# Field-pair products: packed W, end-aligned chunks, one transposed x, and 5120 small memsets on GpSimd

## The chip, the cores and the metric

The kernel runs on one core of one Trainium2 chip. The metric is the device time of one execution in microseconds (us). Engines are named as the profile names them: PE is TensorE's matmul side and PEld its weight loads, DVE is VectorE, ACT is ScalarE, POOL is GpSimd, SP is SyncE. A core has 16 DMA engines.

## The reference

For every batch row there are F = 32 fields of D = 64 numbers. For each of the 496 pairs of fields i < j, field i is multiplied by that pair's own 64 x 64 matrix, and the result is multiplied, element by element, with field j.

```python
i_idx, j_idx = np.triu_indices(32, k=1)          # 496 pairs
vi, vj = inputs[:, i_idx, :], inputs[:, j_idx, :]
vdotw = jnp.einsum('bpd,pde->bpe', vi, W)        # W: (496, 64, 64)
y = (vdotw * vj).reshape(4096, 496 * 64)         # all float32
```

The output has 4096 x 31,744 numbers, 520 MB; x is 33.5 MB and W 8.1 MB.

## The kernel before, in words

The batch is cut into 32 tiles of 128 rows, and everything is done tile by tile (loop over `t`). A tile of x is loaded on ACT's DMA queue into one of two buffers (`load_x`, L82), one tile ahead. TensorE transposes it in two halves of eight 128 x 128 blocks (`transpose_x`, L102), and ScalarE copies each half from PSUM into `xT`, of which there are two (L103). The halves of the next tile are transposed at pairs 5 and 6 of the current one (`PREFETCH_AT`), both halves of the first tile before the loop.

The fields are taken in twos. "Pair p" in the code is fields 2p and 2p + 1, held in the upper and lower 64 partitions of one transposed block. For field i all its products with fields j > i are one wide matmul with (31 - i) x 64 columns. W is packed on the host accordingly: two halves of rows, one for even and one for odd fields. It is loaded on SP's queue in 16 loads into 16 buffers, one for each pair (L115).

A pair's columns are cut from the left into chunks of at most 512. Each chunk takes two of the eight PSUM banks (`take_banks(2)`, four chunks are in flight), one bank for each of the two fields; two matmuls fill them (L145). VectorE multiplies them with the matching columns of x and writes into the output ring. Where it can, one instruction handles both fields as two runs of columns (`runs`, L155); near the ends there is one instruction per field (L164). Because x's matching columns differ by 64 between the two fields, the two runs of x start 64 columns apart.

The ring has 28,160 columns of SBUF for 31,744 output columns of a tile. Each tile makes four stores on SP's queue (`STORES`, L170) of 7552, 6528, 7872 and 9792 columns, in this order; a store's place in the ring is free again when it has landed. The instructions stand on each engine in the order in which the loops name them; waits between engines, and of an engine on its own earlier results, are derived from overlaps of what is read and written.

Of the kernel before, what the change touches and what calls it, by code (L numbers as in the profile page):

```python
# [1 line left out]

# [6 lines left out]

F32 = mybir.dt.float32  # L10
ALU = mybir.AluOpType

P = 128
BANK = 512
BANKS = 8
CHUNK = BANK

STORES = [[0, 1], [2, 3], [4, 5, 6], [7, 8, 9, 10, 11, 12, 13, 14, 15]]
PREFETCH_AT = [5, 6]
RING = 28160  # L20


@with_exitstack
def pair_bilinear_kernel(
    ctx: ExitStack,
    tc: tile.TileContext,
    x: bass.AP,
    w: bass.AP,
    out: bass.AP,
    F: int,  # L30
    D: int,
):

    nc = tc.nc
    B = x.shape[0]
    NT = B // P
    NPR = F // 2

    width = [(F - 1 - i) * D for i in range(F)]
    off = [sum(width[:i]) for i in range(F)]
    woff = [sum(width[0 : 2 * p : 2]) for p in range(NPR)]  # L60
    store_w = [sum(width[2 * p] + width[2 * p + 1] for p in g) for g in STORES]

    const = ctx.enter_context(tc.tile_pool(name="const", bufs=1))
    xtpool = ctx.enter_context(tc.tile_pool(name="xT", bufs=2))
    psum = ctx.enter_context(tc.tile_pool(name="ps", bufs=1, space=bass.MemoryType.PSUM))

    ident = const.tile([P, P], F32, tag="ident", name="ident")
    make_identity(nc, ident)

    def runs(tl, a, b, n):  # L70

        ap = tl[:, a : a + n]
        return bass.AP(ap.tensor, ap.offset, [list(ap.ap[0]), [b - a, 2], list(ap.ap[1])])


    xbuf = [const.tile([P, (F + 1) * D], F32, tag=f"x{b}", name=f"x{b}") for b in range(2)]
    for xb in xbuf:
        nc.gpsimd.memset(xb[:, F * D :], 0.0)  # L78

    def load_x(t):  # L80
        xt = xbuf[t % 2]
        nc.scalar.dma_start(out=xt[:, : F * D], in_=x[ts(t, P), :])  # L82
        return xt

    pring = psum.tile([P, BANKS * BANK], F32, tag="pring", name="pring")
    bank = 0

    def take_banks(n):

        nonlocal bank  # L90
        if bank + n > BANKS:
            bank = 0
        got = pring[:, bank * BANK : (bank + n) * BANK]
        bank = (bank + n) % BANKS
        return got

    def transpose_x(xT, t, xt, g):

        n = 2 * BANK // P
        pt = take_banks(2)  # L100
        for c in range(n):
            nc.tensor.transpose(pt[:, ts(c, P)], xt[:, ts(n * g + c, P)], ident)  # L102
        nc.scalar.copy(xT[:, ts(g, 2 * BANK)], pt)  # L103

    def new_xT(t):
        return xtpool.tile([P, NPR * P], F32, tag="xT", name=f"xT_{t}")

    ring = const.tile([P, RING], F32, tag="ring", name="ring")
    at = 0
    xs = {0: load_x(0)}  # L110

    w_sb = []
    for p in range(NPR):
        wp = const.tile([P, width[2 * p]], F32, tag=f"w{p}", name=f"w{p}")
        nc.sync.dma_start(out=wp, in_=w[:, woff[p] : woff[p] + width[2 * p]])  # L115
        w_sb.append(wp)

    xTs = {0: new_xT(0)}
    for g in range(2):
        transpose_x(xTs[0], 0, xs[0], g)  # L120

    for t in range(NT):
        xt, xT = xs.pop(t), xTs.pop(t)
        if t + 1 < NT:
            xs[t + 1] = load_x(t + 1)
        for s, group in enumerate(STORES):
            if at + store_w[s] > RING:
                at = 0
            osb = ring[:, at : at + store_w[s]]
            at += store_w[s]  # L130
            o0 = off[2 * group[0]]
            for p in group:
                if t + 1 < NT and p in PREFETCH_AT:
                    if t + 1 not in xTs:
                        xTs[t + 1] = new_xT(t + 1)
                    transpose_x(xTs[t + 1], t + 1, xs[t + 1], PREFETCH_AT.index(p))
                for c0 in range(0, width[2 * p], CHUNK):
                    n = [max(0, min(CHUNK, width[2 * p + h] - c0)) for h in range(2)]
                    half = -(-n[0] // BANK) * BANK
                    pm = take_banks(2 * half // BANK)  # L140
                    for b0 in range(0, n[0], BANK):
                        b1 = min(b0 + BANK, n[0])
                        for h in range(2):
                            if b0 < n[h]:
                                nc.tensor.matmul(  # L145
                                    pm[:, h * half + b0 : h * half + b1],
                                    xT[h * D : (h + 1) * D, ts(p, P)],
                                    w_sb[p][h * D : (h + 1) * D, c0 + b0 : c0 + b1],
                                    start=True,
                                    stop=True,  # L150
                                )
                    o = [off[2 * p + h] - o0 + c0 for h in range(2)]
                    xj = [(2 * p + h + 1) * D + c0 for h in range(2)]
                    if n[1] > half - BANK and o[1] + n[0] <= store_w[s]:
                        nc.vector.tensor_tensor(  # L155
                            runs(osb, o[0], o[1], n[0]),
                            runs(pm, 0, half, n[0]),
                            runs(xt, xj[0], xj[1], n[0]),
                            ALU.mult,
                        )  # L160
                    else:
                        for h in range(2):
                            if n[h]:
                                nc.vector.tensor_tensor(  # L164
                                    osb[:, o[h] : o[h] + n[h]],
                                    pm[:, h * half : h * half + n[h]],
                                    xt[:, xj[h] : xj[h] + n[h]],
                                    ALU.mult,
                                )
            nc.sync.dma_start(out=out[ts(t, P), o0 : o0 + store_w[s]], in_=osb)  # L170


# [33 lines left out]
```

## Time and profile before

The median of 12 runs is 1337.9 us (1337.49 to 1338.22). The profiled execution took 1338.14 us, of which the profile's span is 1336.3.

| engine | instructions | busy us | share of span |
|---|---|---|---|
| PE (matmul) | 5376 | 1142.5 | 85% |
| PEld (weight load) | 5376 | 490.5 | 37% |
| DVE | 1344 | 1199.1 | 90% |
| ACT | 65 | 66.1 | 5% |
| POOL | 8 | 0.9 | 0% |

| DMA queue | packets | MB |
|---|---|---|
| q1: stores and W, issued by SP | 20,736 | 528.49 |
| q10: x, issued by ACT | 4608 | 33.56 |
| q8 and q14: instructions | 59 | 0.83 |

Busy time is what an engine spends inside instructions; a share below 100% doesn't say whether the rest was waiting for something that matters. The mean rate of all DMA is 421 GB/s over the span. GpSimd does nothing after the first 1.5 us, in which it makes the identity matrix for the transposes and clears 64 spare columns behind each x buffer.

The page counts 13,084 instructions with semaphore and DMA-issuing ones. Beside the page's groups, the trace keeps for every DMA packet its start, its duration, its size and its queue, but not which of the 16 DMA engines carried it. That can be followed, since one engine's packets follow each other within a few ns.

### The profile page before, as it was taken

What the parts mean: (1) busy time and instruction counts of PE and PEld (TensorE: products, weight loads), DVE (VectorE), ACT (ScalarE), POOL (GpSimd) and SP (SyncE); (2) the same over time, 40 slices, a digit from 0 to 9 for tenths busy, and PEclk for the clock granted to TensorE, in tenths of its full rate; (3) what the DMA queues carried; (4) which work ended last, traced back from release to release, by engine and by line L of the source; (5) the groups of instructions that cost most, each with busy time, mean ns of one, the idle gap of its engine ahead of it and who ended that gap; (6) DMA issues with size and microseconds to landing.
All of it is one profiled execution on the core that took longest, in us unless ns stands there. A gap on an engine that the chain in (4) does not pass through costs nothing. (4 is left out here: it accounts for less than half of the span.)

```text
span 1336.3 us, 13084 instructions
## 1 busy us (share of the span) xinstructions
PE 1142.5 (85%) x5376; PEld 490.5 (37%) x5376; DVE 1199.1 (90%) x1344; ACT 66.1 (5%) x65; POOL 0.9 (0%) x8
## 2 busy tenths in 40 slices
PE   7888888888988889888888899888888888888883
PEld 3333333333333333333333343333333333333331
DVE  5999998988999999899999999989988989999994
ACT  1000000000000000000000000000000000000000
POOL 0000000000000000000000000000000000000000
PEclk9999999999999999999999999999999999999997
DMA  9999999999999999999999999999999999999998
GB/s 393 431 428 430 427 425 426 414 427 430 408 426 426 414 432 426 419 421 420 427 434 413 424 404 443 423 426 411 430 429 415 426 421 415 426 426 430 418 421 368
DMA packets 25403, 562.88 MB, mean 421 GB/s; under 512 B 2944, under 2 KB 3328, under 8 KB 4864
## 3 DMA queue, kind: packets, MB, share of 16 engines
q1 hardware_dynamic: 20736, 528.49, 92.6%
q10 hardware_dynamic: 4608, 33.56, 6.0%
q8 instruction: 42, 0.69, 0.2%
q14 instruction: 17, 0.14, 0.0%
HBM read 41.94 MB, written 520.09 MB: 421 GB/s over the span
## 5 line engine op out<-in xcount | busy, mean ns | idle before, releaser
L155 DVE TENSOR_TENSOR ring<-pring,x 128x1024 f32<-128x1024 f32 (+3 forms) x1088 | 1154.4, 1107 | 117.3 <-DMA out_dram<-ring 70.9
L145 PE MATMUL pring<-w,xT 64*128 64x512 f32 (+4 forms) x4864 | 1074.8, 553 | 145.7 <-DVE ring L155 141.3
L145 PEld LDWEIGHTS pring<-w,xT 64*128 64x128 f32 x4864 | 432.2, 185 | 761.8 <-DVE ring L155 668.3
L103 ACT COPY xT<-pring 128x1024 f32<-128x1024 f32 x64 | 64.8, 1012 | 1197.5 <-PE pring L102 1197.5
L102 PE MATMUL pring<-ident,x 128*128 128x128 f32 x512 | 72.7, 288 | 29.3 <-DMA x<-in_x_dram 28.7
L102 PEld LDWEIGHTS pring<-ident,x 128*128 128x128 f32 x512 | 58.3, 147 | 65.1 <-issue 65.1
L164 DVE TENSOR_TENSOR ring<-pring,x 128x64 f32<-128x64 f32 (+4 forms) x256 | 71.1, 299 | 3.3
L103 ACT ACT_TABLE_LOAD x1 | 1.3, 1283 | 1.7 <-PEq L198 1.7
masks.py:199 POOL TENSOR_SCALAR_AFFINE_SELECT ident<-ident 128x128 f32<-128x128 f32 x1 | 0.3, 294 | 0.0
L78 POOL MEMSET x<- 128x64 f32 x2 | 0.2, 152 | 0.0
masks.py:197 POOL MEMSET ident<- 128x128 f32 x1 | 0.2, 205 | 0.3 <-POOLq L198 0.3
L198 POOL MEMSET const-bfloat16-1.0<- 128x1 bf16 x1 | 0.1, 102 | 0.0
L198 POOL MEMSET const-uint8-127<- 128x1 uint8 x1 | 0.1, 102 | 0.0
L198 POOL MEMSET const-float32-0.0<- 128x1 f32 x1 | 0.1, 99 | 0.2 <-issue 0.2
L198 POOL MEMSET const-float32-1.0<- 128x1 f32 x1 | 0.1, 99 | 0.0
## 6 DMA issues: line engine op xcount, KB each, us to landing
out_dram<-ring SPq DMA_DIRECT2D x32, 4896.0 KB, 18.6
out_dram<-ring SPq DMA_DIRECT2D x32, 3936.0 KB, 17.3
out_dram<-ring SPq DMA_DIRECT2D x32, 3776.0 KB, 19.0
out_dram<-ring SPq DMA_DIRECT2D x32, 3264.0 KB, 19.4
x<-in_x_dram ACTq DMA_DIRECT2D x32, 1024.0 KB, 17.6
w<-in_w_dram SPq DMA_DIRECT2D x1, 992.0 KB, 7.7
w<-in_w_dram SPq DMA_DIRECT2D x1, 928.0 KB, 12.0
w<-in_w_dram SPq DMA_DIRECT2D x1, 864.0 KB, 13.7
```

Of the source, the lines that this page charges most:

```text
L78: nc.gpsimd.memset(xb[:, F * D :], 0.0)
L102: nc.tensor.transpose(pt[:, ts(c, P)], xt[:, ts(n * g + c, P)], ident)
L103: nc.scalar.copy(xT[:, ts(g, 2 * BANK)], pt)
L145: nc.tensor.matmul(pm[:, h * half + b0 : h * half + b1], xT[h * D : (h + 1) * D, ts(p, P)], w_sb[p][h * D : (h + 1) * D, c0 + b0 : c0 + b1 ...
L155: nc.vector.tensor_tensor(runs(osb, o[0], o[1], n[0]), runs(pm, 0, half, n[0]), runs(xt, xj[0], xj[1], n[0]), ALU.mult,)
L164: nc.vector.tensor_tensor(osb[:, o[h] : o[h] + n[h]], pm[:, h * half : h * half + n[h]], xt[:, xj[h] : xj[h] + n[h]], ALU.mult,)
L198: nc = bacc.Bacc("TRN2", target_bir_lowering=False, num_devices=1)
```

## The change

- W goes into one buffer, packed so that the odd field's columns are shifted by 64, and is loaded in five loads of all rows (pairs 0; 1; 2 and 3; 4 to 6; 7 to 15).
- The chunks of a pair are aligned at their ends: the short chunk comes first, then chunks of 512. With the shift, both fields' chunk lies over the same columns of x, and the instruction reads x once for both runs (a step of 0 between the runs). The first chunk's 64 extra columns of the odd field land in ring columns that the pair's last chunk overwrites later. The spare columns behind x are gone.
- There is one transposed x. Its second half is made at pair 3 of the same tile, its first half at pair 9 of the tile before.
- GpSimd writes one spare column, 128 x 1 numbers, four times for each chunk: 40 chunks x 32 tiles x 4 = 5120 memsets. Nothing reads the column.

```diff
-PREFETCH_AT = [5, 6]
+LOADS = [[0], [1], [2, 3], [4, 5, 6], [7, 8, 9, 10, 11, 12, 13, 14, 15]]
+FIRST_HALF_AT, SECOND_HALF_AT = 9, 3
...
-    woff = [sum(width[0 : 2 * p : 2]) for p in range(NPR)]
+    woff = [i % 2 * D + sum(width[i % 2 : i : 2]) for i in range(F)]
...
+    xT = const.tile([P, NPR * P], F32, tag="xT", name="xT")
+    spare = const.tile([P, 1], F32, tag="spare", name="spare")
...
-    for p in range(NPR):
-        wp = const.tile([P, width[2 * p]], F32, tag=f"w{p}", name=f"w{p}")
-        nc.sync.dma_start(out=wp, in_=w[:, woff[p] : woff[p] + width[2 * p]])
+    w_sb = const.tile([P, sum(width[0::2])], F32, tag="w", name="w")
+    for g in LOADS:
+        upto = woff[2 * g[-1]] + width[2 * g[-1]]
+        nc.sync.dma_start(out=w_sb[:, done:upto], in_=w[:, done:upto])
+        done = upto
+    transpose_x(xbuf[0], 0)
...
-                if t + 1 < NT and p in PREFETCH_AT:
-                    transpose_x(xTs[t + 1], t + 1, xs[t + 1], PREFETCH_AT.index(p))
-                for c0 in range(0, width[2 * p], CHUNK):
+                if p == SECOND_HALF_AT:
+                    transpose_x(xt, 1)
+                if p == FIRST_HALF_AT and t + 1 < NT:
+                    transpose_x(xbuf[(t + 1) % 2], 0)
+                first = (width[2 * p] - 1) % BANK + 1
+                for c1 in range(first, width[2 * p] + 1, BANK):
+                    n = first if c1 == first else BANK
+                    c0 = c1 - n
+                    odd = width[2 * p + 1] and c1 > D
+                    pm = take_banks(2)
+                    for _ in range(4):
+                        nc.gpsimd.memset(spare, 0.0)
...
-                    if n[1] > half - BANK and o[1] + n[0] <= store_w[s]:
+                    o = [off[2 * p + h] - o0 + c0 - h * D for h in range(2)]
+                    if odd and (c0 or c1 < width[2 * p]):
                         nc.vector.tensor_tensor(
-                            runs(osb, o[0], o[1], n[0]),
-                            runs(pm, 0, half, n[0]),
-                            runs(xt, xj[0], xj[1], n[0]),
+                            runs(osb, o[0], o[1], n),
+                            runs(pm, 0, BANK, n),
+                            bass.AP(xj.tensor, xj.offset, [xj.ap[0], [0, 2], xj.ap[1]]),
                             ALU.mult,
                         )
```

On the engines: POOL gets 5119 memsets in a row after the identity matrix and one before its last step, each waiting for the one before it; no other engine waits for them. SP issues 11 DMAs less. DVE has 43 products per tile instead of 42.

## The prediction

> **What bounds the kernel now.** I began with the page's slices and its table of DMA queues, because they say whether any engine can be the limit at all.
>
> ```profile
> PE 1142.5 (85%) x5376; PEld 490.5 (37%) x5376; DVE 1199.1 (90%) x1344; ACT 66.1 (5%) x65; POOL 0.9 (0%) x8
> DMA  9999999999999999999999999999999999999998
> q1 hardware_dynamic: 20736, 528.49, 92.6%
> q10 hardware_dynamic: 4608, 33.56, 6.0%
> q8 instruction: 42, 0.69, 0.2%
> ```
>
> No compute engine is full; the 16 DMA engines are, from the first slice to the last but one. 528.5 MB (the output, and W once) and 33.6 MB of x are moved at 421 GB/s. The next question is whether VectorE still has a say. Its timeline of one batch tile and the waits answer that:
>
> ```profile
> 230.89 0.21 DVE L164 TENSOR_TENSOR ring<-pring,x 128x64 f32<-128x64 f32 x1
> 233.65 9.00 DVE L155 TENSOR_TENSOR ring<-pring,x 128x1024 f32<-128x1024 f32 x8 [2.55 <-DMA out_dram<-ring]
> 242.57 0.54 DVE L164 TENSOR_TENSOR ring<-pring,x 128x192 f32<-128x192 f32 x2
> ...
> 255.65 0.23 DVE L164 TENSOR_TENSOR ring<-pring,x 128x64 f32<-128x64 f32 x1
> ```
> ```profile
> DVE ring L155 <- DMA out_dram<-ring: 70.9, 35, 3.0
> ```
>
> Once per tile VectorE stops for some 2.5 us, before the third store group, until the previous tile's largest store has landed. Then it needs 22.2 us (233.65 to 255.87) for groups three and four and issues the next largest store. This is a loop: landing, 22.2 us of products, issue, landing 18.6 us later (the page's median for that store is of this size). It turns in 41 us. Is the loop paced by VectorE or by the transfers? The trace's packet records decide. The sum over one DMA engine per tile is eight rows of each store and of x:
>
> ```
> packet bytes  15 DMA engines  the 16th, while compute runs  the 16th after 1322 us
> 26112          968 ns          982 to 1020 ns
> 30208         1119 ns         1133 to 1161 ns
> 31488         1166 ns         1166 to 1218 ns
> 39168         1448 ns         1472 to 1500 ns                1448 ns
>  8192 (x)      309 ns          309 to 326 ns
> ```
>
> Fifteen engines need 8 x (968+1119+1166+1448+309) = 40.1 us per tile (39.95 us with the 3.5 ns by which packets overlap). The sixteenth needs 0.98 us more. Following its packets end to start, it has work at every tile boundary: it finishes about 3 us after the others, which run dry for about 0.8 us just before the largest store is issued. 39.95 + 0.98 = 40.93 us against issues 41.0 us apart. **One stretched DMA engine paces the program**; the others idle, and VectorE waits.
>
> What stretches it? Its excess comes in steps of about 9.4 ns, 31.7 us over the run, or 2.4 ns for each of the page's 13,084 instructions. By phase of the tile it is 1.6 to 1.9% where 7.5 to 9 instructions start per us, and 3.3 to 3.5% where the transposes bring 13 per us; the correlation over 20 phases is 0.75. After 1322 us, with no instruction left, its packets have full speed. [...]
>
> [...] 9.4 ns per step and 2.4 ns per instruction are four instructions to a step. [...] PE's 10,752 instructions make the 42 packets of q8 (16,384 bytes, 0.95 us each); the other engines fetch 8192 bytes, 309 ns. [...] VectorE here reads PSUM and x; no row of before has GpSimd beside it, so the trace can't say. [...] beside x, a 39,168-byte packet takes 1766 ns, 318 more, one x packet.
>
> **The change, part by part.**
>
> *GpSimd's memsets.* 40 chunks x 32 tiles x 4 = 5120. Nobody reads the spare column, so nothing waits for it. But they are 5120 more records: 5120 x 2.4 ns = **12.3 us** on the pacing engine. Bounds: 0 (if only other engines' records count) and 14 us (at 2.73 ns, the dearest tenth of the run). I take 12.3. Each memset waits for the one before. POOL's bare rows take 99 ns; a wait on its own engine's previous instruction costs VectorE 187 ns of start to start (below), so 0.2 us is likely, 1.0 ms in all. Bounds 0.035 us (POOL's rows start that close without waits) and more than 0.261 us, where 5120 of them outlast the 1336 us span and POOL becomes the bound.
>
> *Their fetch.* 5120 x 64 B (PE's 0.69 MB by 10,752) is 40 packets of 8192 bytes at 309 ns, 12.4 us of one engine. If they are on any engine but the sixteenth they fit in its 0.98 us per tile plus what the sixteenth loses too: 0. On the sixteenth: 12.4 more. Spread over all: 0.8. I take 0, the others are in the range. Two fetches 657 us apart (317 and 974 us; by their spacing SP's) lie on the sixteenth, PE's do not, so engines seem to have their own places.
>
> *W in five loads.* Eleven loads fewer, and with them 11 x 8 rows per DMA engine and 11 completion packets of 9 ns. A packet costs 9 ns over its bytes less the 3.5 overlap: 88 x 5.5 + 99 ns = **-0.6 us** on every engine. SP's 11.6 us of waits between W issues go, but the queue never ran dry there (W's packets end at 27.7 us, the first store was issued at 24.9), so that is worth 0. A coarser load makes pair 3 and pairs 5, 6, 8 to 15 wait for their group: by bytes at 430 GB/s the last lands at 27 us, and pair 7 is first multiplied near 40 us. 0.
>
> *One transposed x.* The transposes keep their number (512) and their copies (64, 1012 ns). Eight instead of sixteen come before the first matmul: the first product starts some 0.6 us earlier; the DMA is busy with W then, so 0. The second half is made at pair 3, before VectorE's wait, the first half of the next tile at pair 9, twelve us later than x's landing, so PE's 28.7 us of waits for x shrink. PE is ahead by four buffers and VectorE waited for it only 17.3 us, 13.4 at the start. On ACT's queue the x load stands ahead of the copy of pair 3, as it did before pair 5. 0.
>
> *Chunks aligned at the end.* VectorE gets 43 instead of 42 instructions a tile and 64 columns less. What matters is the wait on itself. The chain of waits shows it:
>
> ```profile
> 1281.30 4.49 DVE ring L155 x4
> 1285.78 0.04 DVEq L155
> 1285.82 0.04 issue
> 1285.86 3.49 DVE ring L155 x3
> ```
>
> After a short two-run chunk the next instruction waits for its end: a start to start of 1185 ns for 896 columns, 252 ns over the columns' 933, where other chunks have 65 over. So 187 ns, ten times a tile. In the new order the short chunk comes first and the waiting one is the pair's last: for pairs 0 to 6 it is two or three places behind, done by then; only pairs 8, 9, 10 wait at once. In groups three and four eight waits become three: 5 x 0.187 = 0.94 us off VectorE's 22.2 us. Two more instructions (65 ns each) and 128 columns less (133 ns) cancel. That would shorten the loop if VectorE paced it. It doesn't: the cover is the sixteenth engine, which has some 2 us of queue when the largest store is issued. Worth 0 here; VectorE's wait grows by 0.94 + 0.4 us a tile instead.
>
> **Sum.** The profiled run took 1338.14 us (span 1336.3 and 1.84 around it): 1338.14 + 12.3 - 0.6 = 1349.8. The median of the runs, 1337.9, lies 0.24 lower: **1349.6 us**.
>
> **Rivals.**
>
> *B, no change:* POOL's records cost the pacing engine nothing, say because the stretching comes from PE's own instructions (its rate correlates at 0.80). For it: PE makes 82% of all instructions, so the trace can hardly part them. Then 1337.9 - 0.6 = 1337.3.
>
> *C, faster:* VectorE's loop is the bound after all and my packet chain is wrong. The idle stretches of the DMA engines at tile ends sum to 15 us (engine-time over 16, start and tail left out). With 0.94 us less per tile, 30 us over 32 tiles, they close: 1338 - 15 = 1323. It decides if the sixteenth engine is idle at all when the largest store is issued. Against it: its 40.93 of 41.0 us. With the memsets' cost on top, some 1323 to 1336.
>
> *D, slower still:* the fetch is on the pacing engine, 1349.6 + 12.4 = 1362; or each memset takes 0.3 us and POOL ends at 1536; or GpSimd holds VectorE up by 99 ns for each of 43 instructions, 4.3 us a tile, more than its 2.5 + 1.3 of slack, 0.5 x 32 = 16 over 1338.
>
> **How the numbers follow.** The forecast 0.72, within 1346 to 1354; B 0.10; C 0.09; D 0.09. About 0.2% (2.7 us) is what a measurement can tell from no change. Slower 0.81, same 0.10, faster 0.09. The range takes in B and D's lower part: 1337 to 1357.
>
> **What would show it.** Right: POOL some 0.5 ms busy over about 1 ms, the instruction queues 40 packets richer, tile issues 41.4 to 41.5 us apart while memsets run and 41.0 after, the sixteenth engine's packets 3.5 to 4% long instead of 2.4, VectorE's wait for stores from 71 to 110 us or more. Wrong: 41.0 us apart throughout with memsets running (B), 40.5 (C), or PE and VectorE waiting for POOL or a second late DMA engine (D).

## The result, and the profile after

The changed kernel takes 1354.21 us (median of 7 runs, 1354.1 to 1354.4), the kernel before 1337.88 (29 runs): a ratio of 1.0122, interval 1.0113 to 1.0132. So the change costs 16.3 us, where 11.7 were forecast. The profiled execution took 1354.32 us, its span is 1352.5.

From the page of the kernel after: counts and busy time of each engine, two rows of slices, the DMA queues.

```profile
PE 1162.8 (86%) x5376; PEld 553.9 (41%) x5376; DVE 1183.2 (87%) x1376; ACT 66.1 (5%) x65; POOL 507.7 (38%) x5126
POOL 6666666666666666666666640000000000000000
DMA  9999999999999999999999999999999999999998
q1 hardware_dynamic: 19152, 528.49, 91.6%
q10 hardware_dynamic: 4608, 33.56, 5.9%
q8 instruction: 42, 0.69, 0.2%
q14 instruction: 58, 0.48, 0.1%
L146 POOL MEMSET spare<- 128x1 f32 x5120 | 507.1, 99 | 295.1
```

POOL is the only row that is new. Its 5120 memsets of 99 ns have 157 ns from start to start, because each waits for the one before it, and end in slice 24, at 803 us. The bytes of the two data queues are the same, in 1584 fewer packets, and the share of the DMA engines' time that they took barely moves. The bound is where it was: DMA at 9 in every slice but the last.

The end of the memsets at 803 us splits the program in two, and two stretches can be compared with the same stretches of before. First the kernel before, then the kernel after (from:to, length, then busy time of PE, PEld, DVE, ACT and POOL, granted TensorE clock, DMA share, GB/s):

```profile
52.00:804.00 752.00, 655.09 (x3080) 279.75 (x3076) 687.96 (x770) 36.44 (x36) 0.00 (x0) 1.00 0.99 423
845.00:1296.00 451.00, 391.93 (x1850) 167.92 (x1848) 411.85 (x462) 22.27 (x22) 0.00 (x0) 1.00 0.99 423
```
```profile
52.00:804.00 752.00, 653.35 (x3028) 312.41 (x3026) 665.92 (x775) 36.45 (x36) 474.96 (x4795) 0.96 0.98 416
845.00:1296.00 451.00, 397.59 (x1848) 189.29 (x1846) 405.73 (x472) 22.27 (x22) 0.00 (x0) 0.96 0.99 422
```

While memsets run, 416 GB/s are moved instead of 423; afterwards 422. The loss is all in the first stretch. The packet records say it in time. Each tile's largest store starts 41.74 us after that of the tile before it over the first 18 tiles, and 40.85 us over the rest; before it was 40.97 and 40.73. The clock is lower after, 0.96 in both stretches, so with memsets and without; the DMA doesn't follow it.

One engine's packets carry the loss. Summed over the run, the packets of the pacing engine are 46.9 us longer than those of the other fifteen, against 31.7 before: 4.3 us for each 100 us while memsets run, 2.3 to 2.4 afterwards, as much as before.

The timeline of VectorE over one tile of the kernel after (start, length, what ran, and in brackets the wait ahead of it), and its waits for stores (total, times, longest):

```profile
229.14 3.49 DVE L159 TENSOR_TENSOR ring<-pring,x 128x1024 f32<-128x1024 f32 x3
237.29 9.07 DVE L159 TENSOR_TENSOR ring<-pring,x 128x896 f32<-128x896 f32 x9 [4.67 <-DMA out_dram<-ring]
...
258.47 2.21 DVE L159 TENSOR_TENSOR ring<-pring,x 128x896 f32<-128x896 f32 x2
```
```profile
DVE ring L159 <- DMA out_dram<-ring: 120.0, 46, 5.0
```

VectorE's wait ahead of group three is 4.67 us instead of 2.55, and 120.0 instead of 70.9 us in all. From the end of the wait to the end of group four, where the largest store is issued, it is about 21.3 us (237.29 to 258.6), where it was 22.2. VectorE became quicker, and waits longer.

### The profile page after: what moved, and what is told of

Read it like the earlier page. It is cut to its first block, busy times and chain, and to the rows that moved or that the text cites. A ratio compares the mean times of both kernels' runs of the same rounds, so it can differ in the third digit from the quotient of the medians.

```text
span 1352.5 us, 18254 instructions
## 1 busy us (share of the span) xinstructions
PE 1162.8 (86%) x5376; PEld 553.9 (41%) x5376; DVE 1183.2 (87%) x1376; ACT 66.1 (5%) x65; POOL 507.7 (38%) x5126
## 4 chain that ended last, share of the span: by engine, by line
DMA 50%; DVE 33%; issue 9%; PE 6%; POOL 0%; DVEq 0%; ACT 0%; POOLq 0%
DMA out_dram<-ring 50%; DVE ring L159 29%; PE pring L149 6%; DVE ring L167 5%; POOL spare L146 0%; PE pring L107 0%; DVEq L159 0%; ACT xT L108 0%; DVEq L198 0%; POOL ident masks.py:199 0%; DVEq L167 0%; POOL ident masks.py:197 0%; POOLq L194 0%
## 5 line engine op out<-in xcount | busy, mean ns | idle before, releaser
L149 PE MATMUL pring<-w,xT 64*128 64x512 f32 (+4 forms) x4864 | 1100.8, 569 | 161.7 <-DVE ring L159 151.1
L159 DVE TENSOR_TENSOR ring<-pring,x 128x1024 f32<-128x1024 f32 (+3 forms) x1056 | 1104.2, 1106 | 150.3 <-DMA out_dram<-ring 120.0
L149 PEld LDWEIGHTS pring<-w,xT 64*128 64x128 f32 x4864 | 498.4, 194 | 721.8 <-DVE ring L159 534.7
L146 POOL MEMSET spare<- 128x1 f32 x5120 | 507.1, 99 | 295.1
L167 DVE TENSOR_TENSOR ring<-pring,x 128x64 f32<-128x64 f32 (+3 forms) x320 | 97.4, 354 | 1.2 <-DMA out_dram<-ring 0.9
L107 PEld LDWEIGHTS pring<-ident,x 128*128 128x128 f32 x512 | 55.5, 142 | 57.1 <-DVE ring L159 48.8
```

The lines of the kernel that those rows point to most:

```text
L146: nc.gpsimd.memset(spare, 0.0)
L149: nc.tensor.matmul(pm[:, h * BANK : h * BANK + n], xT[h * D : (h + 1) * D, ts(p, P)], w_sb[h * D : (h + 1) * D, a : a + n], start=True, st ...
L159: nc.vector.tensor_tensor(runs(osb, o[0], o[1], n), runs(pm, 0, BANK, n), bass.AP(xj.tensor, xj.offset, [xj.ap[0], [0, 2], xj.ap[1]]), ALU ...
L167: nc.vector.tensor_tensor(osb[:, o[h] + h * D : o[h] + n], pm[:, h * (BANK + D) : h * BANK + n], xj[:, h * D :], ALU.mult,)
```

## The experiments

In all of them "+" and "-" are against the kernel named, and the kernel before ran beside each at 1337.5 to 1337.9 us. Two runs part the memsets from the rest of the change. Theory R of the expectations: every instruction on record in the trace makes the packets of one DMA engine, the one that paces the program, longer, by 2.4 ns on average in the kernel before (31.7 us / 13,084).

**1. The change without memsets.**

```diff
-    spare = const.tile([P, 1], F32, tag="spare", name="spare")
...
-                    for _ in range(4):
-                        nc.gpsimd.memset(spare, 0.0)
```

> The changed kernel without its memsets. Theory R [...]: only the eleven saved W loads are left, 1337.3 us, 0.6 below before; that engine's excess is back to about 32 us. Rival L (the rest of the change costs something too, since 16.3 us were measured for 12.3 forecast): 1340 to 1342 us. Rival C (VectorE's loop paced the kernel before): the shorter loop shows now, 1323 to 1330 us.

Measured: 1338.23 us against 1337.65, ratio 1.0004 (0.9996 to 1.0012). Packed W, aligned chunks and the single transposed x are together worth nothing that shows. VectorE's waits and its largest group in this kernel:

```profile
DVE ring L156 <- DMA out_dram<-ring: 105.2, 41, 4.1
L156 DVE TENSOR_TENSOR ring<-pring,x 128x1024 f32<-128x1024 f32 (+3 forms) x1056 | 1104.4, 1111 | 135.2 <-DMA out_dram<-ring 105.2 <-PE pring L146 19.1
```

The wait for stores is 105.2 us with no memset in the program: it took in what VectorE had gained. That ends rival C: a shorter VectorE loop is not a shorter program. The clock was 0.967 here too, so the memsets don't lower it.

**2. The kernel before, plus memsets.** The same two edits, added to the kernel before.

> The kernel before with the 5120 memsets alone, four for each chunk as in the changed kernel. Theory R: 1337.9 + 5120 x 3.0 ns (the stretch of the pacing engine's packets grew from 31.7 to 46.9 us in the changed kernel) = 1353 us. Rival L: 12.3 us from the memsets, 1350. If the records did nothing: 1338.

Measured: 1354.08 us, ratio 1.0123 (1.0109 to 1.0136): +16.4. The pacing engine's packets were 46.7 us long over the others'. The 16.3 us of the change are the memsets' alone, and the layout around them doesn't matter.

**3. Half of them.** `range(4)` becomes `range(2)`: 2560 memsets.

> The changed kernel with two memsets for each chunk, 2560 instead of 5120, each the same. Theory R: the cost is by the number, so half: 1345.5 to 1346 us, and GpSimd is done after 402 us. A rival in which the mere presence of a busy GpSimd costs [...] would keep the cost per us of GpSimd's activity too, so this run tells R only from a fixed cost (1354 us) and from a threshold (1338 us).

Measured: 1345.96 us, ratio 1.0062 (1.0048 to 1.0076), 7.7 us over experiment 1. The group of memsets:

```profile
L146 POOL MEMSET spare<- 128x1 f32 x2560 | 253.5, 99 | 147.5
```

They end at 402 us. The excess of the pacing engine is 4.3 to 4.4 us per 100 us up to there and 2.3 afterwards. The same rate for half as long, so half the cost.

**4. No wait between memsets.** 128 spare columns take turns, so that a memset depends on none of the recent ones.

```diff
+    spare = const.tile([P, 128], F32, tag="spare", name="spare")
...
+                        nc.gpsimd.memset(spare[:, turn : turn + 1], 0.0)
+                        turn = (turn + 1) % 128
```

> The changed kernel with the 5120 memsets going round 128 spare columns, so that none has to wait for the one before. The number of instructions is the same. Theory R with one record for each instruction: the cost is the same, 1353 to 1354 us, though GpSimd is done far sooner (157 ns apart with the wait, perhaps 35 to 100 without). If the wait or its semaphore is what makes a memset dearer (3.0 ns) than the average instruction before (2.4 ns): 1350 us. If cost follows the time in which GpSimd is active: 1342 to 1347 us.

Measured: 1352.74 us, ratio 1.0113 (1.0099 to 1.0126), 14.5 over experiment 1. POOL's slices and the group of memsets, then two stretches of this kernel, one inside the burst and one after it:

```profile
POOL 8877881000000000000000000000000000000000
L147 POOL MEMSET spare<- 128x1 f32 x5120 | 171.2, 99 | 38.9 <-issue 23.0 <-POOL spare L147 15.9
```
```profile
40.00:200.00 160.00, 132.35 (x602) 66.99 (x604) 132.97 (x157) 7.09 (x7) 128.34 (x3843) 0.93 0.93 394
240.00:1296.00 1056.00, 934.06 (x4338) 436.82 (x4336) 953.23 (x1111) 52.69 (x52) 0.00 (x0) 0.97 0.99 424
```

The memsets start 33 ns apart (171.2 us / 5120), with pauses 41 ns on average, and are done at 211 us. Nearly the whole cost is paid there: 394 GB/s in the burst, 424 after it, with tiles 43 to 46 us apart up to that point. A quarter of the time on GpSimd, 91% of the cost. The cost goes by the **number** of memsets. Their wait on each other can account for the 1.5 us between this run and the changed kernel at most, 0.3 ns each.

**5. A quarter as many, each wider.** One memset of 448 columns for each chunk: 1280 of them.

```diff
-    spare = const.tile([P, 1], F32, tag="spare", name="spare")
+    spare = const.tile([P, 448], F32, tag="spare", name="spare")
...
-                    for _ in range(4):
-                        nc.gpsimd.memset(spare, 0.0)
+                    nc.gpsimd.memset(spare, 0.0)
```

> The changed kernel with one memset of 448 columns for each chunk, 1280 in all, in place of four of one column. GpSimd is busy for longer than in the changed kernel (by the 99 to 205 ns of its rows for 1 to 128 columns, some 0.5 us each, 640 us) and writes 112 times as much. Theory R: only the number counts, 1280 x 3.1 ns over 1338.2 = 1342.2 us. If GpSimd's busy time or its writes cost something: 1354 us or more.

Measured: 1342.31 us, ratio 1.0036 (1.0023 to 1.0048), 4.1 over experiment 1. Two groups of this kernel:

```profile
L158 DVE TENSOR_TENSOR ring<-pring,x 128x1024 f32<-128x1024 f32 (+3 forms) x1056 | 1103.5, 1105 | 139.3 <-DMA out_dram<-ring 106.8 <-PE pring L148 21.4
L145 POOL MEMSET spare<- 128x448 f32 x1280 | 604.3, 472 | 73.3
```

GpSimd is busier than in the changed kernel, 604 us against 507, and writes 112 times as many numbers (448 columns for 4), for a quarter of the cost. VectorE's products have the mean that they had without memsets, 1105 against 1111 ns. So neither GpSimd's time nor what it writes costs anything that shows here.

**6. The same on ScalarE.** The memsets give way to two one-column copies on ScalarE for each chunk, 2560 in all. Rival G of the expectation is a cost that only GpSimd's instructions have.

> The changed kernel with its memsets replaced by copies of one column on ScalarE, two for each chunk (2560), reading one spare column and writing another that nobody reads. It is to be compared with the run that has 2560 memsets (1345.96 us) and with the one that has none (1338.2). Theory R: records cost the same whichever engine makes them, 2560 x 2.4 to 3.1 ns, so 1344 to 1346 us. Rival G [...]: 1338 us. ScalarE gets 80 copies of perhaps 0.3 us a tile, 24 us, beside two of 1 us, so it should not become the bound; if the transposed x comes late, VectorE's waits for PE show it.

Measured: 1534.35 us, ratio 1.1468. The run's end can't answer the question, since ScalarE became the bound. Its slices, its copies and two waits, then ScalarE's timeline from one copy of transposed x to the next but one:

```profile
ACT  7888888888888885000000000000000000000000
L147 ACT COPY spare<-spare 128x1 f32<-128x1 f32 x2560 | 491.4, 192 | 82.1 <-ACT spare L147 2.2
PE pring L150 <- ACT xT L108: 208.6, 20, 12.9
DVE ring L160 <- PE pring L150: 245.8, 46, 13.5
```
```profile
97.30 29.89 ACT L147 COPY spare<-spare 128x1 f32<-128x1 f32 x134
127.09 1.01 ACT L108 COPY xT<-pring 128x1024 f32<-128x1024 f32 x1
128.00 11.80 ACT L147 COPY spare<-spare 128x1 f32<-128x1 f32 x53
...
140.07 18.50 ACT L147 COPY spare<-spare 128x1 f32<-128x1 f32 x83 [0.27 <-ACT spare L147]
158.48 1.00 ACT L108 COPY xT<-pring 128x1024 f32<-128x1024 f32 x1
```

A copy takes 192 ns, and the copies start 223 ns apart. They don't stand on ScalarE in the order of the loops, which name 80 a tile: between one copy of transposed x and the next stand 133 to 136, so some 270 a tile, 60 us of ScalarE's time. All are done at 598 us. TensorE waits for the copy of transposed x behind them, VectorE for TensorE: the tiles come 62 us apart until then and 41 us apart afterwards. Two per chunk in the loops' order would be 18 us a tile (80 x 223 ns, an estimate), so it is the order and not the number that made ScalarE the bound. TensorE waited 208.6 us for ScalarE's copies of transposed x, so here what stood ahead of the awaited instruction counted. Nobody waits for GpSimd's memsets in this way, which is why they could hide everything but their number. The question itself, whether ScalarE's instructions stretch the pacing engine, can be put to the packets; the part on the prediction does so.

**7 to 9. Which DMA engine paces.** x is loaded as 120 and 8 rows. The trace shows 15 and 8 completion packets for the two (23 a tile), where a load of 128 rows has 16. As an estimate from these counts, fifteen engines have eight rows of the first, eight engines one row of the second, and one engine is spared; the first expectation calls it the last one. Which engine it is no trace here shows. If the spared one paced the program, this would be faster.

```diff
-        nc.scalar.dma_start(out=xbuf[t % 2], in_=x[t * P : (t + 1) * P, :])
+        for a, b in ((0, 120), (120, P)):
+            nc.scalar.dma_start(out=xbuf[t % 2][a:b], in_=x[t * P + a : t * P + b, :])
```

> The changed kernel without memsets, and each x tile loaded by two DMAs, of 120 and of 8 rows. [...] Theory R: if the pacing engine is the last one, it has 8 x 0.309 = 2.5 us less a tile and paces no more; the others have 39.95 + 0.3 us and some fetches, so the tile takes 40.3 to 40.6 us and the kernel 1316 to 1325. If the pacing engine is another one, it gets 0.17 to 0.31 us more a tile: 1340 to 1348. Rival C (no single engine paces, but VectorE's loop or the mean of all engines): 1338 us, within 2.

> The kernel before with x loaded in 120 and 8 rows as in the run beside it. Theory R: VectorE's loop of before (22.2 us from the landing of the largest store to the issue of the next) is 0.94 us longer than in the changed kernel. With the late engine relieved the store lands some 3 us sooner, so the loop still has slack and both kernels are within 3 us of each other, 1316 to 1328. If the loop is the next bound, this one is slower than the changed kernel by up to 0.9 us a tile, 1325 to 1338.

> The changed kernel with all its 5120 memsets, and x loaded in 120 and 8 rows. Theory R: the 16 us fall on an engine that has 2.5 us of slack a tile, while the memsets take 0.77 us a tile from it; they cost nothing now, so within 2 us of the run without memsets, if that one is at 1316 to 1325. If the split misses the pacing engine: 1356 to 1364. If the memsets' cost has nothing to do with one engine: 16 us over the run without memsets.

Measured: 1357.5 us on experiment 1 (ratio 1.0146), 1372.84 on the kernel before (1.0259), 1373.36 on the changed kernel (1.0266). The spared engine isn't the one that paces. On experiment 1 tiles come 0.4 us later each, about one x packet (309 ns); the first largest store was issued at 57.7 us instead of 51.3, which is the other part. Between 7 and 9 the memsets cost 15.9 us again. The kernel before suffers more, and two waits of its variant say why:

```profile
PE pring L103 <- DMA x<-in_x_dram: 77.2, 27, 12.6
DVE ring L156 <- PE pring L146: 94.7, 69, 17.8
```

Its transposes of the next x stand at pairs 5 and 6. With x landing later TensorE waits there for 77.2 us (28.7 without this edit), and this time VectorE waits for TensorE. The changed kernel's place for them, pair 9, has the room. What the change does beside the memsets is worth nothing while x is early, and 15.3 us (1372.84 - 1357.5) where x is late; the two waits point to the transposes' place. VectorE's shorter loop could be part of it, and no run takes the two apart.

**10. x unevenly, from the third tile on**, on experiment 1: 112 rows, then 7, 7 and 2. The expectation's engine 7 is one that has seven rows of x a tile, its engines 0 to 6 have one or two rows more than eight. These numbers were the author's assumption; no trace here shows which engine has which rows.

```diff
-        nc.scalar.dma_start(out=xbuf[t % 2], in_=x[t * P : (t + 1) * P, :])
+        rows = ((0, P),) if t < 2 else ((0, 112), (112, 119), (119, 126), (126, P))
+        for a, b in rows:
+            nc.scalar.dma_start(out=xbuf[t % 2][a:b], in_=x[t * P + a : t * P + b, :])
```

> The changed kernel without memsets; from the third tile on x is loaded by four DMAs of 112, 7, 7 and 2 rows. [...] In the run with 120 and 8 rows the pacing engine gained about 0.4 us a tile[...]. Theory R: if it is engine 7, it has 0.31 us less a tile, 30 tiles, 1338.2 - 9 = 1329 us; the next engine has 39.95 + 0.6 + fetches, so little more is to be had. If it is one of 0 to 6: 0.31 to 0.6 us more a tile, 1348 to 1358 us.

Measured: 1348.58 us, ratio 1.0083 (1.0069 to 1.0097), 10.35 over experiment 1, or 0.345 us for each of 30 tiles: about one x row (309 ns) more on the pacing engine, not two and not one less. No version faster than both kernels came out of this.

**11. Half of the matmuls.** Experiment 1 with only the even fields' matmuls; the odd fields' products are made from banks that were cleared once.

> The changed kernel without memsets and without the matmuls of the odd fields: 36 a tile, each of four PE instructions (two weight loads, two matmuls), 4608 instructions less. PSUM is cleared once at the start, VectorE multiplies what stands in the odd banks, and all stores are made, so half the output is not the product. PE was not on the path that sets the end. Theory R: 4608 x 2.4 ns less on the pacing engine, 1338.2 - 11 = 1327 us. If records of PE cost nothing, or the pacing engine is stretched by something else: 1338 us.

Measured: 1964.87 us, ratio 1.469. The run's end can't answer the question: the pace passed to TensorE. Its counts, and one group of this kernel; below it the same group of the kernel before:

```profile
PE 1928.1 (98%) x3072; PEld 902.7 (46%) x3072; DVE 1254.9 (64%) x1377; ACT 66.1 (3%) x65; POOL 0.7 (0%) x6
L147 PE MATMUL pring<-w,xT 64*128 64x512 f32 x1536 | 1394.0, 1066 | 10.3 <-ACT xT L109 5.3 <-DVE ring L157 5.0
```
```profile
L145 PE MATMUL pring<-w,xT 64*128 64x512 f32 x3072 | 820.5, 626 | 113.2 <-DVE ring L155 109.1
```

A 512-column pass of a matmul on 64 rows takes 1066 ns when the field on the other 64 rows is left out, and 626 beside it. Half as many took longer.

**12. More PE instructions.** Experiment 1 with a 64-column matmul ahead of each full one in pairs 4 to 6. The full one writes over it. A matmul is two passes here, each with its weight load: 18 x 32 matmuls are 1152 of each in the counts below, 2304 PE instructions more.

```diff
+                    if p in (4, 5, 6):
+                        for h in range(1 + bool(odd)):
+                            a = woff[2 * p + h] + c0 - h * D
+                            nc.tensor.matmul(
+                                pm[:, h * BANK : h * BANK + D],
+                                xT[h * D : (h + 1) * D, ts(p, P)],
+                                w_sb[h * D : (h + 1) * D, a : a + D],
+                                start=True,
+                                stop=True,
+                            )
```

> The changed kernel without memsets, with an extra matmul of 64 columns ahead of each full one in pairs 4 to 6, which the full one overwrites: 18 a tile, each of four PE instructions (two weight loads, two matmuls), 2304 in all. They stand where PE waits while VectorE waits for the ring, so PE's time should not reach the end; if it does, VectorE's wait for PE shows it. Theory R with one price for all records (3.1 ns as for a memset): 1338.2 + 7.1 = 1345.3 us. Theory R with a lower price for PE's (2.3 ns, what is left of the 31.7 us of before if all other instructions cost 3.1): 1338.2 + 5.2 = 1343.4. If only GpSimd's memsets cost something: 1338 us.

Measured: 1343.25 us, ratio 1.004 (1.0027 to 1.0054), 5.0 over experiment 1; the pacing engine's excess is 35.8 us instead of 31.0. Counts, the new group and VectorE's wait for the line with both kinds of waits in it:

```profile
PE 1194.8 (89%) x6528; PEld 614.6 (46%) x6528; DVE 1183.1 (88%) x1376; ACT 66.1 (5%) x65; POOL 0.7 (0%) x6
L147 PE MATMUL pring<-w,xT 64*128 64x64 f32 x1152 | 110.7, 269 | 61.4 <-DVE ring L166 61.4
DVE ring L166 <- PE pring L156: 35.7, 22, 13.4
```

VectorE waits for TensorE 35.7 us instead of 19.1, but not longer at a time than the 13.4 us of the program's start, and the time lost is found in the packets: 4.8 of the 5.0 us. An instruction on TensorE costs 5.0/2304 = 2.2 ns (1.4 to 2.9 by the ratio's ends), a GpSimd memset 3.1.

## Why the prediction was right, and where its size was off

The forecast was slower, 1349.6 us, within 1337 to 1357. Direction and path held: with 5120 instructions more, the packets of the one DMA engine that sets the pace are 46.9 us longer than the others' instead of 31.7. That GpSimd's instructions are charged at all was in part luck, since the trace of before held only 8 of them and the runs show that not every engine's are. Point by point:

**What bounds the program.** One stretched DMA engine, as read from the packets. Experiments 3, 4 and 12 move its excess by 7.6 us (38.6 - 31.0), put it in a burst, and raise it from TensorE; each time the program's end moves with it. In experiment 4 the rate changes within the burst alone.

**The memsets, 12.3 us.** This is the mis-sized term of the sum. It measured **16.0 us** (1354.21 - 1338.23), 3.1 ns each instead of 2.4. The failed step is the price: 31.7 us were shared out evenly over 13,084 instructions. 82% of those are TensorE's, and experiment 12 prices them at 2.2 ns. So the even share was mainly TensorE's price. As an estimate, 10,752 x 2.2 is 23.7 us, and the 8.0 that remain are 3.4 ns for each of the other 2332; the 1.4 to 2.9 of experiment 12 are too wide to show this. The upper bound of 14 us had the same weakness: its 2.73 ns is the dearest tenth of a run in which TensorE makes most instructions. With 3.1 ns the sum is 1338.14 + 15.9 - 0.6 - 0.24 = 1353.2. The rates told it too late: 41.74 us a tile was measured, where 41.4 to 41.5 stood in the forecast.

**Cost by number.** 1280, 2560 and 5120 memsets cost 4.1, 7.7 and 16.0 us: 3.2, 3.0 and 3.1 ns each. Width, GpSimd's time and the wait on the memset before hardly count.

**Not every engine's instructions.** The prediction charged the same for every instruction, ScalarE's too, and so did theory R in experiment 6. The 7552-column store can test that: its packets of 30,208 bytes take 1119 ns on an undisturbed engine in all five runs of the table. The middle column of the table has the instructions that start in the 9 us that one DMA engine needs for eight such packets. The right column has the excess over 1119 ns, added up over a store's 128 packets (median of the stores; single packets that are over by 100 ns or more are left out).

| experiment | instructions in 9 us | excess per store, ns |
|---|---|---|
| 1, no memsets | 55 TensorE, 10 VectorE | 158 |
| 12 | 101 TensorE, 9 VectorE | 259 |
| 3, while memsets run (8 stores) | 55 TensorE, 9 VectorE, 57 memsets | 396 |
| 11 | 34 TensorE, 6 VectorE | 76 |
| 6, while copies run (9 stores) | 10 TensorE, 1 VectorE, 39 copies | 19 |

46 more TensorE instructions add 101 ns, 2.2 each, and 57 memsets 238. At 2.4 ns the 39 copies on ScalarE would add 94 ns; the whole excess is 19 (eight of the nine stores lie between 0 and 39), so by the median a copy costs 0.5 ns at most. In experiment 11 the DMA engines aren't full either (a DMA share of 0.67 from 52 to 804 us, and 0.75 in experiment 6), and TensorE's instructions still show, 76 ns, so it isn't the slack that hides the copies. Whether copies would cost something beside a busy TensorE isn't shown. In this store a memset costs 4.2 ns instead of the 3.1 of the whole run; why stays open.

**Their fetch, 0.** 40 packets of 8192 bytes came, the 40 that were counted out: q14 has 58 packets where the kernel without memsets has 18. They were nearly all on engines other than the pacing one, so the 0 held. A packet of TensorE's has 256 instructions here (10,752 / 42), one of GpSimd's 128 (5120 / 40).

**The memsets' length, 0.2 us.** 157 ns, and POOL ends at 803 us, well inside the span.

**VectorE and GpSimd.** That this part of D is small was not shown by the trace of before, which has no row with GpSimd beside VectorE's products. The runs show it. VectorE's largest group takes 1106 ns on average in the run with memsets, 1105 with wide ones, 1111 without, and in the two stretches of the changed kernel above all products take 0.86 us on average, beside memsets (665.92 / 775) and after them (405.73 / 472).

**W's packets, -0.6.** Not seen: experiment 1 came out 0.6 us above the kernel before, with an interval of about a microsecond to each side. The packets did go (1584 fewer). Whether their gain was real and something else took it back stays open.

**VectorE's shorter loop, 0.** Right, and for the reason given. The loop lost about 0.9 us, as worked out, and its wait for stores took it: 105.2 us without memsets, 120.0 with.

**A reading of the trace that was wrong.** 1766 ns is not what a 39,168-byte packet takes beside x. Nearly all such packets (328 of 333) are the first of a largest store on their engine, most of them after idle time; beside x the packets take 1448 ns, 2499 of them between two packets of x. So packets of the two queues took turns here one by one, and no sum rested on the 1766.

**Rivals.** B falls with experiments 2, 3 and 12: memsets cost, and so do TensorE's instructions. C falls with experiment 1. D's three parts fall with the fetch, the 157 ns and VectorE's products.

**What stays open.** What it is in an instruction that stretches the packets isn't shown; charging it by the record was the author's assumption. The 9.4 ns steps fit four of TensorE's instructions (2.2 ns each), but only three memsets (3.1), and ScalarE's copies (0.5 ns at most) speak against one price for all engines. Every run here lists a span and a clock, so none shows the kernel unprofiled, and whether the 16 us exist then wasn't tried. A rival for part of the price is the semaphore: in the trace each of the 5120 memsets updates one. TensorE's extra instructions of experiment 12 update none (1533 updates with them and without) and cost 2.2 ns all the same, and each of ScalarE's copies updates one and shows no cost; but the memset's higher price may come from it. Open as well are which of the DMA engines it is, and why the engines' prices differ.

## What to carry to other kernels

Where the DMA engines are full, follow one of them packet by packet before you trust the mean: here the slowest of sixteen set the pace, with 40.93 us of packets a tile where the others had 39.95, and memsets that move no data made it slower still. Price an added instruction by rows of its own kind, not by an average that another engine's instructions make up: here a memset cost 3.1 ns, more than that average of 2.4, and a copy on ScalarE nothing that shows. Count it even on an engine that nobody waits for. And ask of a loop that gets shorter what its end waits for: here the 0.9 us a tile that VectorE saved came back as a wait for stores (105.2 us in the kernel without memsets, 70.9 in the kernel before).

## What the runs showed of the hardware that was not expected

- Memsets on GpSimd, which nobody waits for, and added matmuls, which move no data by DMA either, cost DMA time here: 3.1 ns for each memset and about 2.2 ns for each TensorE instruction, on one of 16 DMA engines. In a burst of memsets 41 ns apart on average the core moved 394 GB/s, and 424 after it. One-column copies on ScalarE showed no such cost: 39 of them beside a store whose excess was 19 ns in all.
- GpSimd starts memsets of one column 157 ns apart when each waits for the last, 33 ns apart in rows in which none does, though both are shown as 99 ns long.
- Matmuls on one 64-row half took longer without those on the other half: 1066 ns for 512 columns, where it was 626 ns with the two in turn in the kernel before; a weight load took 330 and 185 ns in these two.
